# Gated linear attention: output added up column by column in two open PSUM banks, DVE steps moved to ACT, two of eight products moved to GpSimd

## The chip, the cores and the metric

The kernel runs on one core of a Trainium2 chip. It is one program with eight layers, of which this case changes the first, a gated linear attention. The metric is the device time of one execution in microseconds; the median of several runs is given, and one further execution was profiled.

Engines are named as in the profile: PE multiplies matrices (PEld loads its weights), DVE is the vector engine, ACT the scalar engine, POOL the GpSimd engine, SP a queue for transfers. SBUF is the working memory, PSUM the memory of eight banks that PE writes into.

## The reference, cut to what matters

The first layer works on 4 sequences of 1024 tokens of width 128, cut into 16 heads of 8 columns each. All arithmetic is fp32.

```python
def _gla_forward(hidden_states, Wq, Wf, Wi, Wo):       # hidden_states is layernorm(x)
    q = jax.nn.softmax(hidden_states @ Wq, axis=-1)
    k = 1.0 - jax.nn.softmax(hidden_states @ Wf, axis=-1)
    g = jax.nn.log_softmax(hidden_states @ Wf, axis=-1)
    v = hidden_states @ Wi
    ...
    def step(S, inp):                                   # S: (b, head, 8, 8), one step per token
        qt, kt, vt, gt = inp
        S = S * jnp.exp(gt)[..., None] + kt[..., None] * vt[..., None, :]
        ot = jnp.einsum('bhk,bhkv->bhv', qt * SCALE, S)
        return (S, ot)
    ...
    return o @ Wo

x = x + _gla_forward(layernorm(x), ...)
...          # seven more layers: two mixtures of experts, three attentions, two dense layers
```

The exponential of g is the softmax of the f logits itself. So with `a` for that softmax the recurrence is S = a S + (1 - a) v, for each pair of a key column and a value column of a head.

## The kernel before, in words

The residual `x` stays in SBUF as 32 tiles of 128 tokens. `gated_linear_attention` loops over the 4 sequences (`b`, called batches below), each of 8 token tiles. For one batch it does the following.

1. **Softmax part.** `normed` computes the layernorm: statistics on DVE (L90, L91), a square root on ACT (L95), some small DVE steps (L96 to L102) and the normalisation `xn` on DVE (L104). PE transposes the eight tiles into PSUM banks (L80), and `evacuate` copies them to `xnT`, alternately on ACT (L70) and DVE (L72). PE computes the q and f logits, two token tiles to a bank (L155). DVE takes row maxima (L164), ACT exponentials with row sums (L168), DVE reciprocals (L172), the factor for q (L174) and the normalisation of `sm` (L175). The q half and the f half of `sm` are transposed and copied to `qT` and `aT`, and DVE computes `kT` = 1 - `aT` (L181). Key columns now lie on the 128 partitions and the 1024 tokens along the free dimension.
2. **Scan part.** For each of the 8 value columns j of a head, PE computes v in a pair of PSUM banks (L186), already repeated for the eight keys of a head. DVE multiplies it by `kT` into `u` (L194) and runs the recurrence over all tokens, `s` (L196). POOL multiplies `qT` by `s` into column j of `qs` (L197).
3. **Output part.** For each token tile t, PE adds the products of the eight columns of `qs` with `wo_rep` in one PSUM bank (L201), and DVE adds the bank to `x` (L122).

PSUM is cut by `psum("first", 4, 2)`: four single banks (tag `bank`, used for transposes, logits and output tiles) and two pairs of banks (tag `banks`, used for v). Most SBUF tiles have two buffers (`bufs=2`); `qs` has one.

The program is written as plain Python loops. The order of the instructions on each engine is not written out by hand: when the program is built, a list scheduler picks for each engine a ready instruction, the one that stands earliest in the program first, and it places the buffers. The trace shows this: the layernorm statistics of batches 1 to 3 run on DVE between 9.6 and 33.5 us, in gaps of the softmax part of batch 0. Each engine then runs its own list in that fixed order and waits where an input is late.

The layers behind start when the pools of the first layer are closed, that is when its last `x` is written: the mixture of experts has its first DVE instruction at 264.35 us.

Of the kernel before, what the change touches and what calls it, by code (L numbers as in the profile page):

```python
# [13 lines left out]
F32 = mybir.dt.float32  # L14
I32 = mybir.dt.int32
F32R = mybir.dt.float32r
AF = mybir.ActivationFunctionType
ALU = mybir.AluOpType
AX = mybir.AxisListType

P = 128
B, T = 4, 1024
NB = T // P
NT = B * NB
H = 16
DK = P // H
# [8 lines left out]
class Core:  # L35
# [35 lines left out]
        else:  # L71
            self.nc.vector.tensor_copy(out, in_)  # L72

    def transpose(self, dst, srcs):

        for i in range(0, len(srcs), 4):
            part = srcs[i : i + 4]
            ps = self.bank()
            for j, src in enumerate(part):
                self.nc.tensor.transpose(ps[:, j * P : (j + 1) * P], src, self.ident)  # L80
            n = len(part) * P
            self.evacuate(dst[:, i * P : i * P + n], ps[:, :n])

    def layernorm(self, pool, dst, src, n):

        nc = self.nc
        stats = pool.tile([P, n, 6], F32, tag="ln_stats", name="ln_stats")
        mv = pool.tile([P, n, 2], F32, tag="ln_mv", name="ln_mv")
        for t in range(n):
            nc.vector.bn_stats(stats[:, t, :], src[:, t, :])  # L90
            nc.vector.bn_aggr(mv[:, t, :], stats[:, t, :])  # L91
        ve = pool.tile([P, n], F32, tag="ln_ve", name="ln_ve")
        nc.vector.tensor_scalar_add(ve, mv[:, :, 1], EPS)
        r = pool.tile([P, n], F32, tag="ln_r", name="ln_r")
        nc.scalar.activation(r, ve, AF.Sqrt)  # L95
        nc.vector.reciprocal(r, r)  # L96

        c = pool.tile([P, n], F32, tag="ln_c", name="ln_c")
        nc.vector.tensor_mul(c, r, r)
        nc.vector.tensor_mul(c, c, ve)  # L100
        nc.vector.tensor_scalar(c, c, -0.5, 1.5, ALU.mult, ALU.add)
        nc.vector.tensor_mul(r, r, c)  # L102
        for t in range(n):
            nc.vector.tensor_scalar(  # L104
                dst[:, t, :], src[:, t, :], mv[:, t, 0:1], r[:, t : t + 1], ALU.subtract, ALU.mult
            )
# [18 lines left out]
def gated_linear_attention(k: Core, wqf_d, wi_d, wo_rep_d, x_d):  # L125


    nc, tc = k.nc, k.tc
    scale = DK ** (-0.5)
    with tc.tile_pool(name="gla_w", bufs=1) as wp, tc.tile_pool(name="gla", bufs=2) as pool:  # L130
        for b in range(B):
            nc.sync.dma_start(
                k.x[:, b * NB : (b + 1) * NB, :],
                x_d[b].rearrange("(t p) d -> p t d", p=P),
            )
            if b == 0:
                wqf = k.load(wp, "gla_wqf", wqf_d, nc.scalar)
                wi = k.load(wp, "gla_wi", wi_d, nc.scalar)
                wo_rep = k.load(wp, "gla_wo", wo_rep_d, nc.scalar)

        wi_rep = wp.tile([P, DK, P], F32, name="wi_rep")
        cols = wi.rearrange("p (h j) -> p h j", j=DK)
        for j in range(DK):
            nc.gpsimd.tensor_copy(
                wi_rep[:, j, :].rearrange("p (h c) -> p h c", c=DK),
                cols[:, :, j : j + 1].to_broadcast([P, H, DK]),
            )
        for b in range(B):
            xnT = k.normed(pool, b)

            sm = pool.tile([P, NB, 2, P], F32, tag="sm", name="sm")
            for t in range(0, NB, 2):
                ps = k.bank()
                for i in range(2):
                    nc.tensor.matmul(  # L155
                        ps[:, i * 256 : (i + 1) * 256],
                        lhsT=xnT[:, (t + i) * P : (t + i + 1) * P],
                        rhs=wqf,
                        start=True,
                        stop=True,  # L160
                    )
                logits = ps.rearrange("p (g c) -> p g c", c=P)
                nmax = pool.tile([P, 4], F32, tag="nmax", name="nmax")
                nc.vector.tensor_reduce(nmax, logits, AX.X, ALU.max, negate=True)  # L164
                e = sm[:, t : t + 2].rearrange("p t g c -> p (t g) c")
                ssum = pool.tile([P, 4], F32, tag="ssum", name="ssum")
                for g in range(4):
                    nc.scalar.activation(  # L168
                        e[:, g, :], logits[:, g, :], AF.Exp, bias=nmax[:, g : g + 1],
                        accum_out=ssum[:, g : g + 1],  # L170
                    )
                nc.vector.reciprocal(ssum, ssum)  # L172
                rq = ssum.rearrange("p (t g) -> p t g", g=2)[:, :, 0]
                nc.vector.tensor_scalar_mul(rq, rq, scale)  # L174
                nc.vector.tensor_mul(e, e, ssum.unsqueeze(2).to_broadcast([P, 4, P]))  # L175
            qT = pool.tile([P, T], F32, tag="qT", name="qT")
            k.transpose(qT, [sm[:, t, 0, :] for t in range(NB)])
            aT = pool.tile([P, T], F32, tag="aT", name="aT")
            k.transpose(aT, [sm[:, t, 1, :] for t in range(NB)])
            kT = pool.tile([P, T], F32, tag="kT", name="kT")  # L180
            nc.vector.tensor_scalar(kT, aT, -1.0, 1.0, ALU.mult, ALU.add)  # L181
            qs = pool.tile([P, DK, T], F32, tag="qs", name="qs", bufs=1)
            for j in range(DK):
                v = k.banks()
                for c in range(2):
                    nc.tensor.matmul(  # L186
                        v[:, c * 512 : (c + 1) * 512],
                        lhsT=wi_rep[:, j, :],
                        rhs=xnT[:, c * 512 : (c + 1) * 512],
                        start=True,  # L190
                        stop=True,
                    )
                u = pool.tile([P, T], F32, tag="u", name="u")
                nc.vector.tensor_mul(u, kT, v)  # L194
                s = pool.tile([P, T], F32, tag="s", name="s")
                nc.vector.tensor_tensor_scan(s, aT, u, 0.0, ALU.mult, ALU.add)  # L196
                nc.gpsimd.tensor_mul(qs[:, j, :], qT, s)  # L197
            for t in range(NB):
                ps = k.bank()
                for j in range(DK):  # L200
                    nc.tensor.matmul(  # L201
                        ps[:, :P],
                        lhsT=qs[:, j, t * P : (t + 1) * P],
                        rhs=wo_rep[:, j, :],
                        start=(j == 0),
                        stop=(j == DK - 1),
                    )
                k.add_to_x(b * NB + t, ps[:, :P])


class Experts:
# [958 lines left out]
@with_exitstack  # L1170
def kernel(ctx: ExitStack, tc: tile.TileContext, a: dict, out: bass.AP):
    k = Core(ctx, tc)
    dram = ctx.enter_context(tc.tile_pool(name="dram", bufs=1, space=bass.MemoryType.DRAM))
    with tc.tile_pool(name="moe_w", bufs=1) as wp:
        with k.psum("first", 4, 2):
            gated_linear_attention(k, a["gla_wqf"], a["gla_wi"], a["gla_wo"], a["x"])
        with tc.tile_pool(name="ca_pairs", bufs=1) as rows:
            m = Experts(k, wp, a["gateT"], a["gamma"], a["beta"], a["moe_wi"], a["moe_wo"])
            pairs = Pairs(k, rows, dram, "ca", 6, 1)
            with k.psum("moe", 4, 2):  # L1180
                mixture_of_experts(k, m, dram, "0")
            causal_attention(k, pairs, a["ca_wq"], a["ca_wk"], a["ca_wv"], a["ca_wo"])
        with k.psum("second", 4, 2):
            mixture_of_experts(k, m, dram, "1")
    with tc.tile_pool(name="ff_w", bufs=1) as wp:
        f = Dense(k, wp, *(a[n] for n in _DENSE))
        with k.psum("third", 4, 2), tc.tile_pool(name="ra", bufs=1) as pool:
            rotary = Rotary(k, pool, *(a[n] for n in _ROTARY))
            dense_layer(k, f, "0", rotary.pieces)
        with tc.tile_pool(name="aa_pairs", bufs=1) as rows:  # L1190
            pairs = Pairs(k, rows, dram, "aa", H // 2, NEAR)
            alibi_rows(k, pairs, a["aa_qrows"], a["aa_krows"])
            alibi_attention(k, pairs, *(a[n] for n in _ALIBI))
        with k.psum("fourth", 4, 2):
            dense_layer(k, f, "1", None, out)
# [134 lines left out]
```

## Time and profile before

| | us |
|---|---|
| Median of 3 runs | 3002.26 (2995.02 to 3008.82) |
| Profiled execution, its own time | 2999.22 |
| Its span, first to last instruction | 2997.5 |
| First layer in it, start to the last write of x | 0 to 264.44 |
| Batch 2, from its first transpose to that of batch 3 | 144.08 to 203.54, or 59.46 |
| Busy in 144.00 to 203.50: PE, DVE, POOL, ACT | 43.56, 43.90, 26.12, 7.51 |
| Granted PE clock in that stretch | 0.89 |

The profile gives, for groups of instructions, their number, the busy time and the mean duration of one, then the idle time of the engine ahead of them and what ended it. The timeline gives start, duration, engine, line and operation, with equal neighbours merged ("x2"). Two things must be known to read it. An fp32 matrix product appears as two MATMUL records, so the 256 products of L201 are 512 records. And the duration of an instruction on DVE or POOL includes the time in which it has been issued but is held up by another engine.

The first layer is 264.4 of 2997.5 us, or 9% of the span.

### The profile page before, as it was taken

The numbers are of one execution on the slowest core, as the hardware profiler recorded it, in microseconds if no ns is written. First come the engines' busy times: TensorE is split into PE (matmuls) and PEld (weight loads), VectorE is DVE, ScalarE is ACT, GpSimd is POOL, SyncE is SP. The second block draws the span as 40 slices with busy tenths as digits, with TensorE's granted clock in tenths as the row PEclk, the third lists the DMA queues.
The fourth block names the chain that finished last, engine by engine and source line by source line (L and its number), as shares of the span: only waits on it lengthen the run. The fifth ranks groups of instructions, "written<-read, shape, count | busy, mean of one in ns | idle before, by whom it ended". The sixth has DMA issues, their size and how long they took to land. (4 is left out here: it accounts for less than half of the span.)

```text
span 2997.5 us, 40154 instructions
## 1 busy us (share of the span) xinstructions
PE 2270.0 (76%) x14227; PEld 1259.7 (42%) x14227; DVE 1763.1 (59%) x4957; ACT 1131.0 (38%) x1758; POOL 1110.4 (37%) x826
## 2 busy tenths in 40 slices
PE   5774222699999999999413169992799999999898
PEld 3543212344444444443212136671344445454566
DVE  7677401767777767772620275553677777773654
ACT  1110000145454444544101126561155555556675
POOL 4336324067777677777431422324000000000222
PEclk8887557599999999999656689996599999999899
DMA  3000001310111011000001210002321212100000
GB/s 124 1 1 4 10 31 44 115 72 16 30 72 30 16 72 30 16 16 1 1 14 34 75 36 1 0 1 64 109 84 30 76 30 80 35 16 2 4 11 15
DMA packets 62391, 106.33 MB, mean 35 GB/s; under 512 B 12940, under 2 KB 38542, under 8 KB 62178
## 3 DMA queue, kind: packets, MB, share of 16 engines
q1 hardware_dynamic: 50372, 86.23, 9.0%
q10 hardware_dynamic: 7710, 9.00, 0.9%
q0 software_dynamic: 4096, 8.40, 0.9%
q8 instruction: 117, 1.92, 0.3%
q14 instruction: 96, 0.79, 0.1%
HBM read 55.35 MB, written 44.04 MB: 33 GB/s over the span
## 5 line engine op out<-in xcount | busy, mean ns | idle before, releaser
L578 ACT ACTIVATE e<-scores 128x1024 f32<-128x1024 f32 (+3 forms) x704 | 544.9, 792 | 564.9 <-PE scores L466 363.1
L700 POOL TENSOR_TENSOR e_first<-e_first,e 128x1024 f32<-128x1024 f32 (+3 forms) x320 | 538.1, 1718 | 300.7 <-PE o L682 203.5
L488 DVE CUSTOM_DVE_ANT_0 junk<-bank,mask 128x128 f32<-128x128 f32 (+3 forms) x1024 | 493.9, 482 | 213.0 <-PE bank L460 145.8
L493 DVE TENSOR_REDUCE nm<-bank 128x1 f32<-128x512 f32 x512 | 331.1, 685 | 106.4 <-PE bank L460 100.2
L682 PE MATMUL o<-e,v 128*32 128x512 f32 (+3 forms) x2560 | 285.7, 479 | 0.0
L460 PE MATMUL bank<-aa_k,aa_q 62*128 62x512 f32 (+3 forms) x768 | 236.2, 427 | 40.8 <-DVE nm L493 25.9
L846 PE MATMUL o<-e,v 128*32 128x512 f32 (+3 forms) x1536 | 223.3, 508 | 0.0
L460 PE MATMUL bank<-ca_k,ca_q 62*128 62x512 f32 (+3 forms) x768 | 189.6, 414 | 19.8 <-DMA ca_k<-ca_k 11.1
L466 PE MATMUL scores<-halves 64*128 64x128 f32 x2048 | 197.0, 259 | 0.0
L466 PEld LDWEIGHTS scores<-halves 64*128 64x128 f32 x2048 | 190.9, 193 | 9.3 <-issue 0.5
L460 PE MATMUL scores<-ca_q,ca_k 64*128 64x512 f32 (+3 forms) x768 | 181.1, 445 | 4.0 <-ACT e L578 2.4
L817 POOL TENSOR_TENSOR lo<-val,hi 128x512 fp32r<-128x512 f32 x16 | 20.1, 1276 | 423.0 <-ACT hi L816 397.2
L460 PEld LDWEIGHTS scores<-ca_q,ca_k 64*128 64x128 f32 x768 | 77.3, 187 | 228.4 <-ACT e L578 159.1
L460 PE MATMUL scores<-aa_q,aa_k 64*128 64x512 f32 (+3 forms) x768 | 162.9, 407 | 2.7 <-ACT e L578 2.6
L460 PEld LDWEIGHTS bank<-aa_k,aa_q 62*128 62x128 f32 x768 | 119.9, 199 | 105.5 <-DVE nm L493 54.5
L1129 DVE TENSOR_TENSOR h<-val,h 128x512 fp32r<-128x512 f32 x128 | 90.5, 714 | 121.2 <-ACT h L1128 87.6
L375 DVE COPY answer<-bank 128x256 f32<-128x256 f32 x16 | 6.8, 425 | 258.6 <-PE bank L367 258.6
L197 POOL TENSOR_TENSOR qs<-qT,s 128x1024 f32<-128x1024 f32 x32 | 104.5, 3285 | 140.6 <-DVE s L196 140.6
L1073 POOL CAST h<-gate 128x512 fp32r<-128x512 f32 x32 | 26.5, 829 | 337.0 <-DVE gate L1106 331.2
L720 DVE RECIPROCAL raw<-raw 128x128 f32<-128x128 f32 x128 | 117.8, 937 | 56.7 <-ACT raw L716 43.0
L1083 PE MATMUL bank<-h,ff_h1s 128*128 128x512 f32 x512 | 134.2, 407 | 14.3 <-POOL h L1077 10.3
L80 PE MATMUL bank<-ident,given 128*128 128x128 f32 x32 | 6.7, 293 | 174.8 <-DMA given<-slots 174.8
(263 smaller groups left out, 4077.6 us busy)
## 6 DMA issues: line engine op xcount, KB each, us to landing
ca_q<-ca_q SPq DMA_DIRECT2D x64, 128.0 KB
ca_k<-ca_k SPq DMA_DIRECT2D x64, 128.0 KB
aa_q<-aa_q SPq DMA_DIRECT2D x64, 128.0 KB
aa_k<-aa_k SPq DMA_DIRECT2D x64, 128.0 KB
ca_q<-hi SPq DMA_DIRECT2D x8, 512.0 KB
ca_q<-lo SPq DMA_DIRECT2D x8, 512.0 KB
ca_k<-hi SPq DMA_DIRECT2D x8, 512.0 KB
ca_k<-lo SPq DMA_DIRECT2D x8, 512.0 KB
```

The source lines that it names most:

```text
L197: nc.gpsimd.tensor_mul(qs[:, j, :], qT, s)
L460: self.k.nc.tensor.matmul(out, lhsT=lhsT, rhs=rhs, start=True, stop=stop, skip_group_check=True)
L466: self.k.nc.tensor.matmul(ps, lhsT=part[:, 0, :], rhs=part[:, 1, :], start=False, stop=(a == 1), skip_group_check=True,)
L488: nc.vector.tensor_tensor_reduce(junk[:, :cols], ps[:, :cols], self.mask[:, 512 - cols :], -1.0, 3e38, ALU.add, ALU.min, to,)
L493: nc.vector.tensor_reduce(to, ps[:, :cols], AX.X, ALU.max, negate=True)
L578: nc.scalar.activation(e[:, :, :w], ps[:, :, :w], AF.Exp, scale=scale)
L682: nc.tensor.matmul(outs[which][32 * i : 32 * i + 32, skip:], lhsT=v[:, j, i, 32 * which : 32 * which + 32], rhs=es[i // 2][:, i % 2, : 512 ...
L700: nc.gpsimd.tensor_add(to, to, es[i][:, :, : 512 - skip])
L720: nc.vector.reciprocal(part, part)
L846: nc.tensor.matmul(o[32 * i : 32 * i + 32, skip:], lhsT=v[:, j, 4 * r + i, :], rhs=es[i // 2][:, i % 2, : 512 - skip], start=(j == 0), sto ...
L1083: nc.tensor.matmul(ps, lhsT=weights[:, c, :], rhs=inputs[c][i], start=(s == 0), stop=(s == len(steps) - 1))
L1129: nc.vector.tensor_sub(nxt[1][:, o, :], val, hi.bitcast(F32))
```

## The change

The edits all lie in the first layer.

- The output is added up column by column. A pair of banks `out` is opened at the start of a batch. As soon as column j of `s` has been multiplied by `qT`, now in place, the eight products of that column are added into `out`, one for each token tile; four tiles share a bank, and only the first product in a bank has the start flag. One DVE instruction over 1024 columns adds `out` to `x`. `qs` goes away; `s` has four buffers.
- PSUM is cut into two single banks and three pairs.
- The layernorm's last step runs on ACT (with one more small DVE step for its bias), as do all copies after transposes, the normalisation of the softmax (16 instructions of 128 columns instead of 4 of 512), the factor for q, which goes into the copy of `qT`, and `kT`.
- For j = 2 and j = 6, ACT copies v from PSUM to `u` and POOL multiplies `u` by `kT`.

```diff
-    def transpose(self, dst, srcs):
+    def transpose(self, dst, srcs, scale=None):
...
-            self.evacuate(dst[:, i * P : i * P + n], ps[:, :n])
-
-    def layernorm(self, pool, dst, src, n):
+            if scale is None:
+                self.evacuate(dst[:, i * P : i * P + n], ps[:, :n])
+            else:
+                self.nc.scalar.activation(dst[:, i * P : i * P + n], ps[:, :n], AF.Copy, scale=scale)
+
+    def layernorm(self, pool, dst, src, n, scalar=False):
...
+        if scalar:
+            nc.vector.scalar_tensor_tensor(c, mv[:, :, 0], -1.0, r, ALU.mult, ALU.mult)
+            for t in range(n):
+                nc.scalar.activation(
+                    dst[:, t, :], src[:, t, :], AF.Identity, bias=c[:, t : t + 1], scale=r[:, t : t + 1]
+                )
+            return
...
-            xnT = k.normed(pool, b)
+            xn = pool.tile([P, NB, P], F32, tag="xn", name="xn")
+            k.layernorm(pool, xn, k.x[:, b * NB : (b + 1) * NB, :], NB, True)
+            xnT = pool.tile([P, T], F32, tag="xnT", name="xnT")
+            k.transpose(xnT, [xn[:, t, :] for t in range(NB)], 1.0)
...
-                rq = ssum.rearrange("p (t g) -> p t g", g=2)[:, :, 0]
-                nc.vector.tensor_scalar_mul(rq, rq, scale)
-                nc.vector.tensor_mul(e, e, ssum.unsqueeze(2).to_broadcast([P, 4, P]))
+                for g in range(4):
+                    nc.scalar.activation(e[:, g, :], e[:, g, :], AF.Copy, scale=ssum[:, g : g + 1])
...
-            k.transpose(qT, [sm[:, t, 0, :] for t in range(NB)])
+            k.transpose(qT, [sm[:, t, 0, :] for t in range(NB)], scale)
...
-            k.transpose(aT, [sm[:, t, 1, :] for t in range(NB)])
+            k.transpose(aT, [sm[:, t, 1, :] for t in range(NB)], 1.0)
...
-            nc.vector.tensor_scalar(kT, aT, -1.0, 1.0, ALU.mult, ALU.add)
-            qs = pool.tile([P, DK, T], F32, tag="qs", name="qs", bufs=1)
+            nc.scalar.activation(kT, aT, AF.Copy, bias=1.0, scale=-1.0)
+            out = k.banks()
...
-                nc.vector.tensor_mul(u, kT, v)
-                s = pool.tile([P, T], F32, tag="s", name="s")
+                if j % 4 == 2:
+                    nc.scalar.copy(u, v)
+                    nc.gpsimd.tensor_mul(u, kT, u)
+                else:
+                    nc.vector.tensor_mul(u, kT, v)
+                s = pool.tile([P, T], F32, tag="s", name="s", bufs=4)
                 nc.vector.tensor_tensor_scan(s, aT, u, 0.0, ALU.mult, ALU.add)
-                nc.gpsimd.tensor_mul(qs[:, j, :], qT, s)
-            for t in range(NB):
-                ps = k.bank()
-                for j in range(DK):
+                nc.gpsimd.tensor_mul(s, qT, s)
+                for t in range(NB):
+                    cut = slice(t * P, (t + 1) * P)
                     nc.tensor.matmul(
-                        ps[:, :P],
-                        lhsT=qs[:, j, t * P : (t + 1) * P],
-                        rhs=wo_rep[:, j, :],
-                        start=(j == 0),
-                        stop=(j == DK - 1),
-                    )
-                k.add_to_x(b * NB + t, ps[:, :P])
+                        out[:, cut], lhsT=s[:, cut], rhs=wo_rep[:, j, :], start=(j == 0 and t % 4 == 0),
+                        stop=(j == DK - 1), skip_group_check=True,
+                    )
+            rows = k.x[:, b * NB : (b + 1) * NB, :].rearrange("p t d -> p (t d)")
+            nc.vector.tensor_add(rows, rows, out)
...
-        with k.psum("first", 4, 2):
+        with k.psum("first", 2, 3):
```

## The prediction

> **What bounds the kernel now.** I read the page first: the change touches lines that run only in the first 264 us, so the later layers count only through the moment at which they start. Then the windows by batch, the groups, and the timeline of one batch.
>
> The windows (length, busy time of PE, PEld, DVE, ACT, POOL, then the PE clock):
>
> ```profile
> 0.00:33.00 33.00, 14.11 (x48) 9.85 (x48) 24.47 (x131) 14.69 (x44) 3.99 (x21) 0.95 0.90 280
> 144.00:203.50 59.50, 43.56 (x203) 30.18 (x202) 43.90 (x44) 7.51 (x35) 26.12 (x8) 0.89 0.00 1
> 203.50:264.40 60.90, 44.20 (x202) 29.78 (x201) 44.47 (x46) 7.52 (x35) 26.21 (x9) 0.86 0.00 0
> ```
>
> A batch takes 59.5 us and no engine is busy for more than 44 of them. ACT does nearly nothing. The groups of the layer:
>
> ```profile
> L197 POOL TENSOR_TENSOR qs<-qT,s 128x1024 f32<-128x1024 f32 x32 | 104.5, 3285 | 140.6 <-DVE s L196 140.6
> L196 DVE TENSOR_TENSOR_SCAN s<-aT,u 128x1024 f32<-128x1024 f32 x32 | 93.5, 2962 | 0.0
> L194 DVE TENSOR_TENSOR u<-kT,banks 128x1024 f32<-128x1024 f32 x32 | 37.8, 1208 | 3.1 <-PE banks L186 3.0
> L266 POOL TENSOR_TENSOR x<-x,n 128x1024 f32<-128x1024 f32 x4 | 9.4, 2345 | 8.8 <-DVE n L104 8.8
> ```
>
> POOL's multiply takes 3.29 us here, but the same kind and shape takes 2.35 us in L266. So it is held up. The timeline of batch 2 shows by what:
>
> ```profile
> 174.40 1.22 DVE L194 TENSOR_TENSOR u<-kT,banks 128x1024 f32<-128x1024 f32 x1 [0.48 <-PE banks L186]
> ...
> 179.34 2.26 DVE L196 TENSOR_TENSOR_SCAN s<-aT,u 128x1024 f32<-128x1024 f32 x1
> 179.49 6.55 POOL L197 TENSOR_TENSOR qs<-qT,s 128x1024 f32<-128x1024 f32 x2 [2.23 <-DVE s L196]
> ...
> 181.52 2.32 DVE L194 TENSOR_TENSOR u<-kT,banks 128x1024 f32<-128x1024 f32 x2
> 183.78 6.59 DVE L196 TENSOR_TENSOR_SCAN s<-aT,u 128x1024 f32<-128x1024 f32 x2
> ...
> 188.27 6.54 POOL L197 TENSOR_TENSOR qs<-qT,s 128x1024 f32<-128x1024 f32 x2 [2.23 <-DVE s L196]
> ...
> 194.86 8.84 PE L201 MATMUL bank<-gla_wo,qs 128*128 128x128 f32 x72 [0.22 <-POOL qs L197]
> ...
> 203.74 0.29 DVE L122 TENSOR_TENSOR x<-x,bank 128x128 f32<-128x128 f32 x1 [1.50 <-PE bank L201]
> 204.61 0.69 DVE L72 COPY xnT<-bank 128x512 f32<-128x512 f32 x1 [0.59 <-PE bank L80]
> ```
>
> POOL starts at 179.49 and at 188.27: 8.78 us for two columns, 4.39 for one. A free scan takes 2.26 us, or about 2.2 from start to start. POOL's two multiplies begin at 179.49, but the first gets going only when the scan ends at 181.6, for 6.55 - 2.1 = 4.4 us are left, 2.2 for each. The next scan, issued at 183.78, waits until POOL is done at 186.04. So scans and POOL multiplies **exclude each other**: 2.2 + 2.2 = 4.4, the whole period. The products `u` (1.2 us) run beside POOL at no cost.
>
> So a batch has three serial pieces. From the first transpose (144.08) to the first `u` (157.29): 13.2 us, the softmax part. From there to POOL's end (194.81): 37.5 us, of which 8 x 4.39 = 35.1 are the exclusion. From there to the next batch's first transpose (203.54): 8.7 us, in which PE does the 36 products (72 records) that came too late for the four single banks. The next batch's softmax cannot start earlier: its transposes want single banks, which stand behind the output tiles. In the trace batch 1's `xn` is ready at 20.5, yet it is transposed at 81.77.
>
> **What the Trainium skill says.** *SBUF — State Buffer*, "Who interferes with whom": a DVE instruction with two SBUF inputs excludes a GpSimd one that reads SBUF, the later issued fully blocks; one with a single SBUF input and no 2-port mode does not, and ACT never waits. The trace agrees: scan against `qs` 4.4 us a pair, `u` (second input in PSUM) 2.32 us for two beside a running POOL. *ScalarE: Activation LUTs*, "What ACT_TABLE_LOAD costs": 186 ns + 0.833 ns per element, 93 more for each pointer operand, 93 overlapped between neighbours. The trace has 586 ns for a 512-column copy, where that gives 613. The same page, "Table sets": copy and identity are in every set, so no table load is added; no run here shows it yet.
>
> **Part by part, per batch.**
>
> *Output by column.* The 64 products stay the same. But after the last `qs` only column 7 is left: 8 products or 16 records at 8.84/72 = 0.123, 2.0 us instead of 8.8. The eight L122 (0.29 each) become one add that I price like L194, 1.2. The single banks no longer serve the output, so the next batch's softmax may run **beside** the scans. That is worth more than the tail: up to 13.2 + 8.7 us per batch.
>
> *ACT.* It gains, as estimates from the skill's prices (spacing, after overlap): 8 `xn` with two pointers at 0.39, 16 normalisations with one at 0.29, `kT` and two copies of v (1024 columns, 1.04 each); from the trace, three more half copies at 0.58 less overlap. 3.1 + 4.7 + 3.1 + 1.5 = 12.4, with the 7.5 of before 20 us of 40: not a bound. If the pointer forms do not overlap (0.48, 0.39), 22.
>
> *DVE.* It loses `xn` 2.7, L174 and L175 3.4, copies and `kT` 2.8, two `u` 2.4, adds 1.1. Left are 8 scans (17.6), 6 `u` (7.0), maxima and reciprocals (3.1), the add (1.2), statistics and small steps (about 5): 34 us. What went was either two-input or from SBUF, so it also leaves the exclusion.
>
> *POOL.* Two more multiplies: 10 x 2.2 = 22. Here the edit **costs**: they read SBUF, so they stand in the exclusion, while the two `u` that they replace stood outside it. Excluded time per batch: (8 + 10) x 2.2 = 39.6 against 35.1. The least that they may cost is nothing, if DVE were the bound; the most is 2 x 2.35 plus the wait of a scan for the chain copy, multiply.
>
> *PE.* v: 32 records at 0.43 (3.60 us for 8 at 86.60) is 13.8; output 128 x 0.123 = 15.7; logits 3.7; transposes 3.1: 36.3 at full clock. At the 0.86 to 0.89 granted now the page has 43.6 to 44.2 busy. So PE is close behind.
>
> *Start.* Batch 0 has nothing to hide behind. `u` begins at 33.42 now. ACT's exponentials start about 1 us later (two `xn` prices), the 16 normalisations add 4.7 to its 5.5, copies and `kT` about 1.5 against DVE's share: about 39, with bounds 36 and 43.
>
> **The sum.** Start 39, first `u` 1.2, four periods P, the end 2.0 + 1.2. With P = 39.6 (exclusion always in use, as now in the scan part: 35.25 from the first scan to the last POOL end against 35.1) the layer ends at 201.8. I take P = 43.5: the order on each queue is fixed at build time, ACT's copies of v stand behind exponentials, PE is at 36 to 44, and v has two pairs of banks with `out` holding one. End: 39 + 1.2 + 174 + 3.2 = 217.4, against 264.4: **47 us gained**. The next layer's DVE work starts within 0.1 us of this end, and its weights were loaded in the first 33 us, so the gain goes through whole. 2999.2 - 47 = 2952 for the profiled execution; the median lies 3 us above it: **2955**.
>
> **Rivals.**
>
> 1. *No overlap.* DVE's list never has room for the maxima of the next batch until its scans are done. For: a scheduler that prefers earlier work, and a DVE with 34 us of it. Against: `u` has two buffers and two of its values now come through ACT and POOL, so DVE's list has gaps, and the trace shows gaps of 0.2 us filled with later work (9.6 to 33 us). Then: 39 + 4 x (1.2 + 39.6 + 3.2) + 3 x about 16 of an ACT-bound softmax part = 263: no change, 3000.
> 2. *Full overlap.* P = 39.6: end 201.8, 62.6 gained, 2940. PE's clock would have to rise to nearly 1 as its gaps close.
> 3. *Slower, one mechanism:* the softmax chain on ACT becomes serial. It decides once nothing overlaps and a batch's ACT chain, 20 to 22 us, is passed through in single steps (copy, POOL multiply, scan) because copies of v stand behind exponentials that wait for DVE: two detours of about 1 + 2.2 + 2 us per batch on top of rival 1, 4 x 10 = 40, less what runs beside: 3020 to 3040. For: ACT is in order. Against: a batch's own copies come long after its own exponentials.
>
> That the change does nothing is excluded by the 8.7 us tails, but rival 1 gives them back.
>
> **How the numbers follow.** A difference under 0.5% (15 us) could not be told from none here. Forecast case, gain 30 to 58: 0.58. Full overlap: 0.10. Half overlapped, gain 15 to 30: 0.10. Rival 1 (within 15): 0.12. Slower: 0.10. Faster 0.78, same 0.12, slower 0.10. Range 2934 (rival 2 and a clock that helps) to 3000 (rival 1).
>
> **What would show it.** Right: POOL's multiplies of 10 columns a batch with the scans fill the layer, and exponentials (L168) lie inside the scan part of the batch before; the layer ends at 205 to 235; PE's clock rises over 0.9. Wrong: ACT idle through the scans and exponentials only after the last scan (rival 1); POOL idle under `u` waiting for ACT (rival 3). If taking the two products back to DVE changes nothing, the price of the exclusion is wrong.

## The result, and the profile after

The change makes the kernel **slower**, by half a per cent. The median is 3016.59 us against 3001.45 us before, 18 runs each; the ratio is 1.0047, with a 95% interval from 1.0033 to 1.0061. The forecast of 2955 us, and its range, were wrong.

The profiled execution after spans 3014.7 us, before 2997.5. The layer that was changed ends at 285.57 us (the last add to `x`, 284.35 + 1.22) instead of 264.44: **21.1 us later, where the prediction had 47 us earlier**. What follows the layer takes 2729.1 us after and 2733.1 before. Over the thirteen kernels of this study this rest, in which all execute the same code, lies between 2716 and 2750, so single spans scatter by some 15 us, and the end of the layer is the cleaner measure of a change in the layer. It is used below.

First the windows by batch of the kernel after, cut at its first `u` and shortly behind its adds (length, busy time of PE, PEld, DVE, ACT, POOL, PE clock):

```profile
0.00:35.00 35.00, 15.92 (x50) 10.14 (x50) 13.41 (x89) 23.05 (x74) 4.00 (x21) 0.90 0.72 212
35.00:95.20 60.20, 41.77 (x184) 31.21 (x185) 32.40 (x35) 23.55 (x74) 29.00 (x10) 0.83 0.08 31
95.20:157.50 62.30, 42.80 (x207) 30.77 (x206) 30.14 (x23) 18.40 (x62) 28.91 (x10) 0.89 0.00 0
157.50:220.70 63.20, 45.22 (x201) 33.29 (x200) 30.24 (x23) 16.88 (x58) 28.53 (x10) 0.81 0.00 1
220.70:285.60 64.90, 38.98 (x162) 29.15 (x160) 27.44 (x16) 3.96 (x5) 30.09 (x12) 0.76 0.00 0
```

The work did move: DVE is busy for about 30 us of a batch instead of 44, ACT for 17 to 24 instead of 7.5 (in the last batch, which has no next one to prepare, for 4). Yet a batch became longer, 63.2 against 59.5 for batch 2. No engine is busy for more than 45 of 63 us, and DVE now waits for half of the time. For whom is in the groups of the layer (busy, mean ns of one, then idle time ahead and what ended it):

```profile
L214 POOL TENSOR_TENSOR s<-qT,s 128x1024 f32<-128x1024 f32 x32 | 96.9, 3042 | 155.7 <-DVE s L213 146.7 <-DVE ssum L186 9.0
L219 PE MATMUL banks<-gla_wo,s 128*128 128x128 f32 x512 | 92.0, 356 | 75.1 <-POOL s L214 75.1
L213 DVE TENSOR_TENSOR_SCAN s<-aT,u 128x1024 f32<-128x1024 f32 x32 | 75.8, 2391 | 28.6 <-POOL u L209 28.2
L211 DVE TENSOR_TENSOR u<-kT,banks 128x1024 f32<-128x1024 f32 x24 | 29.2, 1217 | 73.9 <-PE banks L199 57.1 <-ACT kT L194 16.0
L209 POOL TENSOR_TENSOR u<-kT,u 128x1024 f32<-128x1024 f32 x8 | 18.8, 2353 | 0.0
```

The row to read first is L211. In the kernel before, `u` waited 3.1 us in the whole layer; now it waits 73.9, of which 57.1 for v out of PE. The scans (L213) look better at first sight, 2391 ns instead of 2962. That is no gain: a scan is held up by POOL only while both have work, and now they take turns because one of them has none. These shares are new: 28.2 in which a scan waits for `u` from POOL, 57.1 for v, and 16.0 for `kT`, which now comes from ACT.

Why PE, busy for 43 of 62 us, is late with v shows in the timeline of all engines in batch 1, columns 0 to 2 (start, duration, engine, line):

```profile
101.12 2.28 DVE L213 TENSOR_TENSOR_SCAN s<-aT,u 128x1024 f32<-128x1024 f32 x1
...
103.57 2.35 POOL L214 TENSOR_TENSOR s<-qT,s 128x1024 f32<-128x1024 f32 x1 [14.42 <-DVE s L213]
...
105.97 3.55 PE L219 MATMUL banks<-gla_wo,s 128*128 128x128 f32 x16 [2.04 <-POOL s L214]
...
109.36 6.17 PE L199 MATMUL banks<-xnT,wi_rep 128*128 128x512 f32 x14
...
111.28 1.22 DVE L211 TENSOR_TENSOR u<-kT,banks 128x1024 f32<-128x1024 f32 x1 [4.39 <-PE banks L199]
...
112.54 2.29 DVE L213 TENSOR_TENSOR_SCAN s<-aT,u 128x1024 f32<-128x1024 f32 x1
...
115.00 2.35 POOL L214 TENSOR_TENSOR s<-qT,s 128x1024 f32<-128x1024 f32 x1 [9.08 <-DVE s L213]
117.30 2.35 POOL L209 TENSOR_TENSOR u<-kT,u 128x1024 f32<-128x1024 f32 x1
...
119.69 4.47 DVE L213 TENSOR_TENSOR_SCAN s<-aT,u 128x1024 f32<-128x1024 f32 x2 [3.53 <-POOL u L209]
```

Follow it downwards: it is **one chain through all four stages**. Scan of column 0, POOL's multiply, PE's output products of column 0, and only then PE's v for column 1, `u`, the scan of column 1. From one scan to the next 11.4 us pass, where scan and multiply alone took 4.4 in the kernel before. Nothing in the data asks for this: v is computed from `xnT` alone, from which v of column 0 had already been made. It is PE's list that has v of column 1 behind the output products of column 0. The last four lines show the second wait: POOL takes its list in order too, so the product of column 2 stands behind the multiply of column 1, and the scan of column 2 behind both, 7.15 us after the scan before it.

PE's clock has a share in the chain as well. The output products of column 0 took 3.55 us, those of column 1, at 117.40, took 2.05. The windows around the two (length, busy times as above, then the granted clock) tell them apart, 0.53 against 1.00:

```profile
105.97:109.36 3.39, 3.39 (x16) 3.39 (x17) 0.18 (x1) 3.27 (x17) 0.00 (x0) 0.53 0.00 0
117.40:119.30 1.90, 1.90 (x17) 1.90 (x18) 0.00 (x0) 0.00 (x0) 1.90 (x1) 1.00 0.00 0
```

So of the 7.0 us that the 11.4 have beyond scan and multiply, 1.5 are the clock. The other 5.5 are what the order puts into the chain: the products, v and `u`, one after the other.

PE's list for one batch (here batch 0), as built, reads: v of column 0; output of column 0; v of columns 1, 2, 3 and half of 4; output 1; the rest of v 4; output 2, 3, 4; v of 5, 6, 7; output 5, 6, 7. In the list of the kernel before, the first output products come behind the v of column 3, and 53 of 64 behind the last v.

### The profile page after: what moved, and what is told of

Its sections match the earlier page's. It is cut to its first block, busy times and chain, and to the rows that moved or that the text cites. A ratio compares the mean times of both kernels' runs of the same rounds, so it can differ in the third digit from the quotient of the medians.

```text
span 3014.7 us, 40135 instructions
## 1 busy us (share of the span) xinstructions
PE 2270.9 (75%) x14227; PEld 1268.6 (42%) x14227; DVE 1705.3 (57%) x4845; ACT 1179.5 (39%) x1876; POOL 1122.0 (37%) x834
## 5 line engine op out<-in xcount | busy, mean ns | idle before, releaser
L476 PE MATMUL bank<-aa_k,aa_q 62*128 62x512 f32 (+3 forms) x768 | 234.7, 426 | 41.9 <-DVE nm L509 26.4
L214 POOL TENSOR_TENSOR s<-qT,s 128x1024 f32<-128x1024 f32 x32 | 96.9, 3042 | 155.7 <-DVE s L213 146.7
L219 PE MATMUL banks<-gla_wo,s 128*128 128x128 f32 x512 | 92.0, 356 | 75.1 <-POOL s L214 75.1
```

The source lines that it names most:

```text
L214: nc.gpsimd.tensor_mul(s, qT, s)
L219: nc.tensor.matmul(out[:, cut], lhsT=s[:, cut], rhs=wo_rep[:, j, :], start=(j == 0 and t % 4 == 0), stop=(j == DK - 1), skip_group_check=True,
L476: self.k.nc.tensor.matmul(out, lhsT=lhsT, rhs=rhs, start=True, stop=stop, skip_group_check=True)
```

## The experiments

Eleven kernels. "End" is the end of the changed layer in the profiled execution; the ratio is the time against the kernel before, run on the same chip, with its 95% interval. On the chips of runs 1 to 4, 5 to 8 and 9 to 11 the kernel before took 3006.93, 3002.09 and 2996.00 us, so medians of different groups can't be compared directly, but ratios can. Each end comes from one execution, and how much it scatters from one execution to the next was not measured; the gains that follow from the ratios agree with those of the ends within 10 us in all rows, so differences of a few us between ends should not be leaned on.

| | kernel | end, us | median, us | ratio |
|---|---|---|---|---|
| | before | 264.44 | 3001.45 | 1 |
| | the change | 285.57 | 3016.59 | 1.0047 (1.0033 to 1.0061) |
| 1 | change, sums in a PSUM pool of their own | 280.0 | 3019.72 | 1.0041 (1.0024 to 1.0058) |
| 2 | change, all products on DVE | 271.16 | 3010.37 | 1.0001 (0.9977 to 1.0025) |
| 3 | change, v written two columns ahead | 261.21 | 3001.48 | 0.9975 (0.9959 to 0.9991) |
| 4 | 2 and 3 together | 244.25 | 2983.58 | 0.992 (0.9889 to 0.995) |
| 5 | before, split of products alone | 281.56 | 3021.48 | 1.0063 (1.0049 to 1.0077) |
| 6 | before, output by column alone | 265.66 | 3006.38 | 1.0004 (0.9981 to 1.0028) |
| 7 | 4, softmax part between the columns | 211.09 | 2941.40 | 0.9794 (0.9749 to 0.9839) |
| 8 | 7 with the split | 234.18 | 2971.08 | 0.9869 (0.9836 to 0.9901) |
| 9 | before, moves to ACT alone | 277.84 | 3006.09 | 1.0039 (1.0023 to 1.0054) |
| 10 | 7, v of the next batch ahead as well | 198.45 | 2932.12 | 0.9761 (0.9704 to 0.9818) |
| 11 | 7 without the moves to ACT | 221.41 | 2952.98 | 0.9864 (0.9824 to 0.9905) |

Three theories stood against each other. **A**: the order of PE's list, v behind output products. **B**: the two products on GpSimd, by the exclusion of scans and POOL multiplies and by the detour copy, multiply, scan. **C**: the softmax part, now longer on ACT.

### 1. Are v and the sums in each other's way in PSUM?

```diff
-            out = k.banks()
+            out = k.sums()          # a pool of its own: one pair
...
-        with k.psum("first", 2, 3):
+        with k.psum("first", 2, 2, 1):
```

> The changed kernel, with the pair of banks for the output sums in a pool of its own (two single banks, two pairs for v, one pair for the sums), so that v of columns 0 and 1 need not wait for the first product into the sums. Theory A (PE runs its list in order, and in it v of a later column stands behind the output products of earlier columns; the scans wait for v): PE's list now begins a batch with v of two columns, so the 9 us between the first and the second scan of a batch go; the layer ends near 262 instead of 285.6, the time falls by 15 to 25 us to about 2995. Theory B (the two products on GpSimd: exclusion of 4.4 us a batch and the chain copy, multiply, scan of 4.9 us twice a batch): nothing moves here, 3015. Theory C (the softmax part on ACT is what a batch waits for): nothing moves, 3015.

The layer ended 5.6 us earlier, not 20 and more, although PE's list did now begin a batch with v of two columns. `u` still waits for v:

```profile
L218 DVE TENSOR_TENSOR u<-kT,banks 128x1024 f32<-128x1024 f32 x24 | 28.8, 1213 | 63.2 <-PE banks L206 43.9 <-ACT kT L201 19.1
```

43.9 us remain of 57.1. So banks that `out` takes from v are not the cause of most of the wait; this form of theory A fell. What was left of it is the order itself, which runs 3 and 4 change.

### 2. The two products back on DVE

```diff
-                if j % 4 == 2:
-                    nc.scalar.copy(u, v)
-                    nc.gpsimd.tensor_mul(u, kT, u)
-                else:
-                    nc.vector.tensor_mul(u, kT, v)
+                nc.vector.tensor_mul(u, kT, v)
```

> The changed kernel, with all eight products u on DVE (no copy of v on ACT, no multiply on GpSimd); PE's list keeps the same order of v and output products. Theory A: the waits for v stay; only the wait of the scans for GpSimd's u (28.2 us in all, of which about 18 were GpSimd's own turn) goes: gain 10 to 25 us, the layer ends near 265 to 275. Theory B: this is the cause, the layer ends at 240 or earlier, 40 us gained. Theory C: at most 5 us.

14.4 us earlier, or 3.6 a batch, and still 6.7 behind the kernel before: inside the 265 to 275 of theory A and far from the 240 of theory B, which explains 14.4 us and no more. The groups say what is left:

```profile
L209 DVE TENSOR_TENSOR_SCAN s<-aT,u 128x1024 f32<-128x1024 f32 x32 | 80.6, 2537 | 1.1
L207 DVE TENSOR_TENSOR u<-kT,banks 128x1024 f32<-128x1024 f32 x32 | 38.1, 1213 | 75.6 <-PE banks L199 60.1 <-ACT kT L194 15.5
```

The scans wait no more (1.1 instead of 28.6), but the wait for v is as long as ever, 60.1.

### 3 and 4. v written ahead

```diff
+            for j in range(2):
+                value(j)                       # the matmuls of v, column j
+            out = k.banks()
             for j in range(DK):
...
+                if j + 2 < DK:
+                    value(j + 2)
                 s = pool.tile([P, T], F32, tag="s", name="s", bufs=4)
```

> The changed kernel, with v of column j+2 written in the program ahead of the scan and the output products of column j (v of columns 0 and 1 before the first). Nothing else is changed: same instructions, same banks. Theory A: no scan waits for v any more, both the 9 us after the first scan and the 9 us before the sixth go down to the exclusion of 4.4 us a column; about 10 to 13 us a batch, the layer ends at 235 to 250, the time is 2965 to 2980 and faster than before the change. Theory B: at most 5 us. Theory C: at most 5 us, the batch still ends with an idle DVE and POOL while ACT finishes the softmax.

> Both edits, v written ahead and all eight products on DVE. Theories A and B together: the excluded time is 8 x 4.4 = 35 us a batch, the half of the softmax part that does not overlap adds about 10: the layer ends at 215 to 230, 2950 to 2960. If the two products on GpSimd only cost where v is late (theory A alone), this is within 5 us of the run with v ahead alone.

24.4 us earlier with the split, 41.3 with all products on DVE. This changes no operation, no engine and no number of buffers, only the place of v in the program (and `out` is opened behind the first two v). In run 3 the wait for v is gone from the groups:

```profile
L218 DVE TENSOR_TENSOR u<-kT,banks 128x1024 f32<-128x1024 f32 x24 | 28.5, 1201 | 18.9 <-ACT kT L194 18.9
L222 DVE TENSOR_TENSOR_SCAN s<-aT,u 128x1024 f32<-128x1024 f32 x32 | 95.4, 2992 | 31.1 <-POOL u L216 30.4
```

The other two waits stayed, `kT` 18.9 and POOL's `u` 30.4, and the scans are back at 2992 ns: scans and multiplies now really stand in each other's way. The effects nearly add, 24.4 + 14.4 = 38.8 against 41.3. The granted clock does not explain the gain: over the four batches it was 0.83, 0.89, 0.81 and 0.76 in the change and 0.74, 0.88, 0.85 and 0.82 in run 3, about 0.82 in the mean of both. Theory A is shown as an ordering of the list, yet both runs ended later than it had asked (235 to 250, 215 to 230). The timeline of run 4 shows where: at the end of each batch.

```profile
126.59 3.42 DVE L218 TENSOR_TENSOR_SCAN s<-aT,u 128x1024 f32<-128x1024 f32 x1
135.64 1.22 DVE L229 TENSOR_TENSOR x<-x,banks 128x1024 f32<-128x1024 f32 x1 [5.62 <-PE banks L224]
137.16 0.69 DVE L178 TENSOR_REDUCE nmax<-bank 128x4 f32<-128x512 f32 x1 [0.30 <-PE bank L169]
...
146.72 2.35 DVE L214 TENSOR_TENSOR u<-kT,banks 128x1024 f32<-128x1024 f32 x2 [4.49 <-ACT kT L194]
```

From 130.0 to 146.7 DVE runs no scan. Half of the next batch's row maxima come only after the add, because PE's logits for them stand behind the last output products. It looks like the same fault once more, one stage earlier, and runs 7 and 8 test it: the softmax part lies beside the scans only by half.

### 5, 6 and 9. Each part alone on the kernel before

```diff
+                if j % 4 == 2:                 # run 5
+                    nc.scalar.copy(u, v)
+                    nc.gpsimd.tensor_mul(u, kT, u)
...
-            qs = pool.tile([P, DK, T], F32, tag="qs", name="qs", bufs=1)      # run 6
+            out = k.banks()
...
-        with k.psum("first", 4, 2):
+        with k.psum("first", 2, 3):
...
-            nc.vector.tensor_scalar(kT, aT, -1.0, 1.0, ALU.mult, ALU.add)     # run 9, with xn, sm and all copies
+            nc.scalar.activation(kT, aT, AF.Copy, bias=1.0, scale=-1.0)
```

> The kernel before with one part of the change alone: the products of columns 2 and 6 by a copy on ACT and a multiply on GpSimd. Layer end of before 264.4 us. Theory B (the exclusion of scans and GpSimd multiplies): two more excluded multiplies of 2.2 us a batch, and two scans that wait for copy and multiply, 4.4 to 9.8 us a batch in four batches: layer end 282 to 303. If the price seen between the changed kernel and its copy with all products on VectorE (14.4 us) is what the split costs anywhere: 279. If the split costs only where the next batch waits anyway: 264 to 268.

> The kernel before with another part alone: the output added up by column in two open banks (normalisation, layernorm and copies as before, all products on VectorE). It keeps TensorE's list of v behind the output products of earlier columns. The tail of 8.7 us a batch becomes about 3.2: if nothing took its place, 4 x 5.5 less: layer end 242. Theory A (v behind output products): what the changed kernel with all products on VectorE shows, gaps of about 9 us twice a batch: 4 x 16 more: layer end 258 to 275, near the 271.2 of that kernel. Theory C (the softmax part on ACT is the cause): well under 264, near 242.

> The kernel before with only the moves to ACT (layernorm's last step, normalisation of the softmax, copies after the transposes, 1 - a); output at the end of a batch by token tile, all products on VectorE. Nothing of a batch lies beside the next one, so the softmax part stands alone. Theory C (that part is now set by ACT): in the changed kernel first u starts 1.6 us later than before in batch 0 and the part is 13.2 us in the kernel before; ACT's prices (8 x 0.39 + 16 x 0.30 + 1.05 + half copies) against VectorE's share give 2 to 6 us a batch more: layer end 272 to 288. If ACT is not what the part waits for: 262 to 267.

*Run 5*: 17.1 us later, 4.3 a batch. The end of 281.56 lies between the 282 at which theory B's range began and the 279 that a fixed price of 14.4 us would give, and does not decide between them. The price shows in a new wait: the scans stand for 21.0 us until POOL's `u` is there. *Run 9*: 13.4 us later. In batch 2 the time from the last add to the first `u` is 16.4 us (150.00 to 166.39) against 13.0 before (144.28 to 157.29), so here theory C holds: when nothing lies beside the softmax part, moving it to ACT makes it longer. *Run 6* is the telling one. Output by column was to save 5.5 us a batch, and it saves nothing: 265.66, inside the range of theory A. The saving is there, and is handed over to a wait that the kernel before hardly has (3.1 us):

```profile
L194 DVE TENSOR_TENSOR u<-kT,banks 128x1024 f32<-128x1024 f32 x32 | 38.0, 1209 | 49.2 <-PE banks L186 49.2
```

The kernels form a chain in which each differs from the one before it by one part: output by column +1.2 (before to run 6), the moves to ACT +5.5 (run 6 to run 2), the split +14.4 (run 2 to the change). The sum is the 21.1 by construction, and the prices hold in this order only: the moves alone cost more (13.4), where nothing of the softmax part lies beside the scans.

### 7 and 8. The overlap that the prediction had counted on

The softmax part of batch b+1 is written as a generator, and one piece of it (two token tiles, or one set of transposes) between two columns of batch b.

```diff
+        def softmax(b, made):
...
             for t in range(0, NB, 2):
+                yield
...
             for j in range(DK):
+                next(coming, None)             # coming = softmax(b + 1, made)
                 v = vs.pop(j)
```

> The changed kernel with all products on VectorE, v two columns ahead (as in the run that ended the layer at 244.2), and the softmax part of batch b+1 written piece by piece between the columns of batch b. That run had about 16.7 us at each of three boundaries between batches in which no scan ran. Theory A extended (order of the in-order lists is all that holds the batches apart): three boundaries shrink to 2 to 4 us: layer end 198 to 210, time 2940 to 2955, scans and GpSimd multiplies 35 of each 38 to 41 us. If the softmax part is held by ACT's own work or by TensorE's rate instead: 225 to 244.

> The same with two of eight products on GpSimd as in the change. Theory B: with everything overlapped the exclusion is the bound, so two more excluded multiplies cost their 4.4 us a batch in full, and more where a scan waits for copy and multiply: layer end 15 to 35 us later than with all products on VectorE. If the split is free once TensorE's order is right, within 4 us of it.

Run 7 ends at 211.09, 1.1 us outside the 198 to 210 of theory A and far from the 225 to 244 of its rival: the batches are now 43.8, 43.3 and 42.2 us long from add to add. With the split in, 234.18, **23.1 us later**. So the split costs least where the kernel waits for other things (14.4) and most where nothing else is in the way. The timeline of run 8 shows its price in one place:

```profile
93.99 3.52 DVE L234 TENSOR_TENSOR_SCAN s<-aT,u 128x1024 f32<-128x1024 f32 x1
...
97.68 2.34 POOL L235 TENSOR_TENSOR s<-qT,s 128x1024 f32<-128x1024 f32 x1 [2.32 <-DVE s L234]
99.98 2.35 POOL L228 TENSOR_TENSOR u<-kT,u 128x1024 f32<-128x1024 f32 x1
...
102.36 2.29 DVE L234 TENSOR_TENSOR_SCAN s<-aT,u 128x1024 f32<-128x1024 f32 x1 [4.85 <-POOL u L228]
```

Scan, multiply, product, scan, with no overlap: the product adds its whole 2.35 us to the chain of DVE and POOL. 23.1 us over eight such products are 2.9 each; some of them are themselves held up (2.84 us in the mean), and POOL waits for ACT's copy for 1.8 us in all.

### 10. The last boundary

```diff
-                if j + 2 < DK:
-                    value(j + 2)
+                value(b * DK + j + 2)          # runs on into the next batch
...
+                if j == 0:
+                    out = k.banks()            # opened behind the multiply of column 0
```

> The kernel with the softmax part written between the columns (layer end 211.1), and v of the next batch's columns 0 and 1 written ahead of the output of columns 6 and 7, as for all other columns. That run has 10.0 us from the last GpSimd multiply but one at a boundary to the next batch's first, where 4.65 is the rhythm of the other columns. Theory A (order): the boundary shrinks to 4.7 to 7 us: three boundaries of 2.5 to 5 us: layer end 196 to 204. If the add of the output or TensorE's rate sets the boundary: 207 to 212.

198.45, as theory A had it. From POOL's multiply of column 7 to that of the next column 0 it was 10.04 us in run 7 (119.96 to 130.00) and is 4.66 now (117.89 to 122.55). The time is 2932.12 us, a ratio of 0.9761 to the kernel before. This is **the version that beats both** the kernel before and the change; from run 7 only the end of the layer tells it apart, for the intervals of the two ratios overlap. Its POOL and DVE take turns without a gap:

```profile
90.78 2.31 DVE L232 TENSOR_TENSOR_SCAN s<-aT,u 128x1024 f32<-128x1024 f32 x1
...
93.24 2.36 POOL L233 TENSOR_TENSOR s<-qT,s 128x1024 f32<-128x1024 f32 x1 [2.29 <-DVE s L232]
...
95.34 2.40 DVE L232 TENSOR_TENSOR_SCAN s<-aT,u 128x1024 f32<-128x1024 f32 x1
...
97.89 2.36 POOL L233 TENSOR_TENSOR s<-qT,s 128x1024 f32<-128x1024 f32 x1 [2.29 <-DVE s L232]
```

One column takes 4.65 us, all of it the exclusion: DVE's scan, then POOL's multiply, and the scan issued at 95.34 ends 2.14 us after the multiply. The windows of its batches 1 and 2, add to add:

```profile
89.60:128.20 38.60, 36.53 (x203) 26.71 (x202) 33.04 (x26) 15.31 (x55) 18.84 (x9) 0.96 0.00 1
128.20:165.40 37.20, 33.92 (x193) 24.96 (x191) 33.52 (x26) 14.23 (x53) 18.87 (x9) 1.00 0.00 1
```

37.2 us is 8 x 4.65. DVE is busy for 33.5 and PE for 33.9, so neither is the bound by itself, though neither is far from it; the bound is what two engines cannot do at once.

### 11. What the moves to ACT are worth once everything overlaps

The moves of run 9 are undone in run 7.

> The kernel with the softmax part written between the columns, with the moves to ACT undone (normalisation, layernorm, 1 - a on VectorE, copies shared as before). VectorE gets about 10 us a batch more in a batch of 43 us in which it is busy 34. Were VectorE's sum the bound, layer end 225 to 245; if the moves to ACT bring nothing even here: 207 to 215. Batch 0 alone, in which nothing overlaps, would start 1.6 us or more earlier.

221.41, between the two ranges and 10.3 us later than run 7. The moves cost 13.4 us where nothing overlaps and bring 10.3 where the softmax part lies beside the scans. Part of what they bring is room in the exclusion. `kT` on DVE takes 0.69 us in batch 0 with POOL idle; in batch 1 it is issued beside POOL's multiply and ends 0.55 us after it:

```profile
78.98 2.34 POOL L229 TENSOR_TENSOR s<-qT,s 128x1024 f32<-128x1024 f32 x1 [4.15 <-DVE s L228]
79.52 2.35 DVE L195 TENSOR_SCALAR kT<-aT 128x1024 f32<-128x1024 f32 x1
```

## Why the prediction was wrong, point by point

**The step that failed is the period of a batch, P = 43.5 us, and in it the 3.9 us allowed for the order of the queues.** The batches took 59.5 (from the first `u`), 63.0, 63.2 and 64.9 us, 250.6 together, where the sum had 1.2 + 174 + 3.2 = 178.4. That is 72.2 too little; the start was 4.0 better than forecast (34.99 against 39), and 72.2 - 4.0 = 68.2 is the difference between the layer ends of 285.57 and 217.4. The first of the reasons given for 43.5 was "the order on each queue is fixed at build time"; it and three others shared 3.9 us above the exclusion's 39.6. The order was named and its price was guessed. With the split kept, as predicted, it cost 24.4 us for v (the change to run 3) and 27.0 more for the softmax part (run 3 to run 8): 51.4 of the 68.2, or 12.8 a batch. The other 16.8 remain with the order mended: in run 8 the batches still took 47.0 to 49.5 us. Part of that is the exclusion itself, which was sized at 4.4 us a column and measures 4.65 in run 10; 18 turns of half of that are 41.9 instead of 39.6. The rest was not broken down.

**What was overlooked** is in the text of the prediction itself: the output products were counted for what they save behind the last column, 8.8 - 2.0, but not for what they do ahead of it. A step that is moved forward brings its wait along. Each group of products waits for POOL, and what stands behind it on an in-order engine waits too. In the kernel before, 53 of 64 products stood behind the last v, where the wait held up no v. Run 6 shows that this alone eats the 5.5 us a batch.

**Right: the exclusion.** The Trainium skill, *SBUF — State Buffer*, "Who interferes with whom", says that a DVE instruction with two SBUF inputs and a GpSimd instruction that reads SBUF shut each other out, and that the later one waits in full. Run 10 shows it at its barest, 2.29 and 2.36 us in turn. The least price of the split, two multiplies of 2.2 us or 4.4 a batch, compares with 4.3 in run 5, 3.6 in the change and 5.8 in run 8. That the first is so close is in part luck, since there the scans mostly wait for POOL's `u` instead of being held up. "If taking the two products back to DVE changes nothing, the price of the exclusion is wrong" did not come about. One reading beside it was wrong: not all that left DVE was "two-input or from SBUF", for the copies after transposes and the two `u` read PSUM. For `kT`, which reads SBUF, run 11 bears it out.

**Right: the prices on ACT.** By *ScalarE: Activation LUTs*, "What ACT_TABLE_LOAD costs", 128 columns with one and with two pointer operands come to 386 and 479 ns; the trace has 391 for the normalisation (L188) and 482 for `xn` (L110). No table load was added: the layer has six before and four after. That ACT's busy time would be no bound was right as well: 17 to 24 us of 62. But its steps are passed through one after the other, and where nothing lies beside them that cost 3.4 us a batch (run 9). The start, priced 5.6 us later for them, came only 1.6 later (34.99 against 33.42).

**Wrong: that the softmax part would lie beside the scans.** It does so in part. In the change, three of the four row maxima for batch 2 lie early in batch 1 (100.52, 103.32 and 103.99 us). The logits for the fourth stand between output products in PE's list, and it comes behind the last scan, with the rest of the softmax part after it:

```profile
145.16 4.48 DVE L213 TENSOR_TENSOR_SCAN s<-aT,u 128x1024 f32<-128x1024 f32 x2 [3.53 <-POOL u L209]
...
149.55 0.67 DVE L178 TENSOR_REDUCE nmax<-bank 128x4 f32<-128x512 f32 x1
...
162.19 2.28 DVE L213 TENSOR_TENSOR_SCAN s<-aT,u 128x1024 f32<-128x1024 f32 x1
```

For 12.5 us no scan runs. In run 4 it is half of the maxima that come late, after the add. "The single banks no longer serve the output" was a needed condition and was taken for a sufficient one. Rewritten for it (run 7) the layer ends at 211.09, ahead of the 217.4 forecast, but without the split; with the split kept (run 8) it ends at 234.18.

**Wrong: the PE clock.** It was to rise over 0.9; it was 0.76 to 0.89 in the batches, in the windows above. It rose to 0.96 and 1.00 in batches 1 and 2 of run 10.

**The rivals.** Rival 1, no overlap, had the layer end at 263; rival 3, slower, at 3020 to 3040 us. The result of 3016.59 lies between. Rival 3's mechanism, two detours a batch through copy, multiply, scan, was there but smaller: a scan waits 3.5 us for each product (28.2 over eight) instead of 5.2, and taking the products back gained 1.8 for each. Its reason was wrong too: the copies did not stand behind exponentials; in the timeline POOL's product stands behind POOL's own multiply. The main mechanism, PE's list, was in no rival. Why the list comes out so, with v behind products that are ready later, lies in how it is made and was not tried; shown is only that the place in the program moves it.

## What to carry to other kernels

When a step moves earlier, ask what will stand behind it on its engine: products that wait for a slow chain must come after the work that feeds that chain, and where the order is made from the program text, write the feeding work some steps ahead and interleave the next round's preparation by hand. Do not count a saving at the end of a stage until the in-order lists of the next stage have been read for work placed behind it. Do not give an engine work that shuts out the one on the critical path, however idle it looks: POOL was busy for 26 of 59.5 us and still had no room.

## What the runs showed of the hardware that was not expected

- The granted clock of a batch is a mean of very different stretches. In batch 1 of the change it was 0.89, but 0.53 while PE made the output products of column 0 (3.55 us for sixteen records) and 1.00 for those of column 1 (2.05 us). In batch 0 the products of columns 0, 1 and 2 took 3.57, 2.05 and 3.64 us at 0.53, 1.00 and 0.52. The waits of PE ahead of the two groups of batch 1 were almost the same, 2.04 and 1.86 us; why one stretch was granted less was not tried.
- A multiply of two SBUF operands at 128 x 1024 fp32 on POOL and a scan of the same size on DVE take nearly the same time undisturbed, 2.35 and 2.29 us, and for the length of a column their sum counts.
- The mean duration of an instruction that is excluded by another engine can fall when the kernel gets worse: the scan took 2962 ns before, 2391 after and 2708 in run 10. The shortest scan took 2258, 2264 and 2233 ns, so the mean tells how long scans were held up, not how fast the engine is.
